# Second-pass attention products in four 32-column tiles, layer-1 sums of 24 batches beside the LSTM, and a reserve of two buffers in a four-layer graph network on one core

## The chip, the core and the metric

The kernel runs on one NeuronCore of a Trainium2 chip. The core has a matrix engine (TensorE, "PE" in the profile, its weight loads apart as "PEld"), VectorE ("DVE"), ScalarE ("ACT"), GpSimd ("POOL"), and a queue of its own for issuing transfers (SyncE, "SP"). [...] The metric is the device time of one launch in microseconds, lower is better. A profile is of one execution; its span is the time from its first to its last instruction.

## The reference

The input is 32 independent graphs ("batches") of 512 nodes with 128 features, each with a symmetric 0/1 adjacency of 512 x 512 that has ones on its diagonal. Four layers follow one another, each as `x = x + layer(relu(layernorm(x)), adj)`:

```
layer 0  q, k, v = relu(h Wq + bq), relu(h Wk + bk), relu(h Wv + bv)
         x += softmax(where(adj, q k^T, -9e15)) v
layer 1  conv   = conv1d(last 128 nodes of h) + bias               # 128 steps of 128 features
         lw     = lstm(conv), 128 steps, run over all 32 batches at once
         A_norm = D^-1/2 (adj + 1) D^-1/2,  D from the row sums of adj + 1
         x += sigmoid((A_norm h) lw)
layer 2  four inner layers on n0 = h:
         n' = tanh([norm_rows(adj)^T (n ws + bs), n wn + bn, norm_cols(adj)^T (n wd + bd)] wu + bu)
layer 3  x += prelu(adj (h W) + bias)
```

The LSTM needs layer 0 of the last 128 nodes of all batches, and everything from layer 1's gate `sigmoid((A_norm h) lw)` on needs the last step of the LSTM. The product `A_norm h` doesn't need it.

## The kernel before, in words

The file holds a general kernel and a fast one (`symmetric`) for symmetric adjacencies; the fast one runs here, and the general one only if a flag at the end says so. What follows is the fast one.

It works in three passes over the 32 batches. **Pass 1** (`pass_1`) does layer 0 for the last 128 nodes of each batch, with the convolution, and stores keys, queries, values and the updated rows in DRAM. **The LSTM** (`lstm`) then runs 128 steps over all batches together; beside it, **pass 2** (`pass_2`) does layer 0 for the other 384 nodes. For the batches in `EARLY` (0 to 19) pass 2 also loads the whole adjacency, squares it on ScalarE (the square of 0/1 entries is the same, and the row sums come with it), and computes layer 1's product `A_norm h` (`sums_of_1`), which it stores in DRAM. **The rest** (`rest`) does, for each batch, the layer-1 gate, layer 2 and layer 3; a batch that isn't early computes its sums of layer 1 there, and an early one loads them into a tile `f_gT3` with the tag "gs". The last four batches (`LATE = 4`) have pass 2 ranked with the rest. Two batches, 26 and 27 (`FIRST`), go first in the rest and keep what pass 2 loaded.

The tiles that the prediction names are: `f_z`, the LSTM's gates before tanh; `f_pq`, `f_s`, `f_e`, `f_po`, pass 2's queries, scores, exponentials and weighted sums; `f_pg`, layer 1's sums (and layer 3's); `f_plw` and `f_pl`, the transposed LSTM output and the product with it (the gate); `f_py`, `f_pa`, layer 2's products, with the node tiles `f_n`; `f_xn`, `f_hT`, a normalized batch and its transposition; `f_dgT` and `f_gT3`, the stored and the loaded sums.

All float32 products of a wide stationary operand use the whole 128 x 128 array. The LSTM's products are different: with 32 batches, h is only 32 columns wide as the stationary operand, so `products` (line 1210) issues four matmuls for one step, each into 32 partitions of the output, that is into a 128 x 32 part of the array ("128*32" in the profile). The sums over the adjacency (`aggregate`, line 1396) run in a reduced float32 format at 512 columns.

The order of the work is not written by hand. Every operation is given to a planner (`Plan`) with an engine, an assumed duration, a rank, and the tiles that it reads and writes; `Plan.run` then places operations one by one where they can start first, with a lower rank first among those that can start at once, and keeps each engine's order as planned. The LSTM's operations have ranks below 1000 and are never to be delayed by others on their engine (`held`). For TensorE the planner adds a pause wherever a tiled and an untiled operation follow each other:

```
SWITCH = (0.2, 0.1)                      # line 536: to untiled, to tiled
s = max(s, free[e] + self.SWITCH[o.tiled])
```

An operation can only be placed when buffers for its new tiles are free (`room`, line 663): for each tag it counts how many the operation needs. "gs" has five buffers, the adjacency "a" two, PSUM ("mm") eight banks. The transfers are issued on SP in the planned order, so a transfer that waits for its buffer holds up those behind it; the copy of the squared adjacency to DRAM is issued on POOL.

Lines that matter: 1292 (`f_pq`), 1301 (`f_s`), 1310 (`f_po`), 1213 (`f_z`), 1349 (squares), 1396 (sums), 1432 (load of `f_gT3`), 775 (`EARLY`).

Of the kernel before, what the change touches and what calls it, by code (L numbers as in the profile page):

```python
# [13 lines left out]
P = 128  # L14
# [478 lines left out]
class Cell:  # L493


    def __init__(self, pool, tag, shape, dtype, name, whole=False, filled=False):
        self.pool, self.tag, self.shape, self.dtype, self.name = pool, tag, shape, dtype, name
        self.whole, self.filled = whole, filled
        self.size = 1
        for n in (shape or ())[1:]:  # L500
            self.size *= n
        self.place = None
        self.marked = True
        self.real = None
        self.left = 0
        self.free_at = 0.0
        self.parts = {}
# [13 lines left out]
class Plan:  # L521
# [74 lines left out]
    def run(self, tc, queues):  # L596
# [66 lines left out]
        def room(o):  # L663

            at = 0.0
            need = {}
            for c in o.cells:
                if c not in seen:
                    if c.tag in self.fifo and self.fifo[c.tag][turn[c.tag] + need.get(c.tag, 0)] is not c:
                        return None  # L670
                    need[c.tag] = need.get(c.tag, 0) + 1
            for t, n in need.items():
                spare = n + (t == self.banks and o.rank >= self.spared and self.left > 0)
                if len(slots[t]) < spare or len(slots[t]) == spare and t in self.kept and by_rank and o.rank > by_rank[-1].rank + 12:
                    return None
                at = max(at, sorted(slots[t])[n - 1])
            return at
# [5 lines left out]
        tiled = False  # L683
# [69 lines left out]
def symmetric(ctx, tc, x, adj, weights, cols, rows, lstm_b, prelu_a, out, fail):  # L753
# [18 lines left out]
    MANY = 512 // (4 * B)  # L772
    LATE = 4
    FIRST = [B - LATE - 2 + k for k in range(2)]
    EARLY = range(20)
    FOLDS = (4, 7, 10, 13)
    MOVED = range(2, B - 2)
    TURN = 32
# [34 lines left out]
    def t_mm(n):  # L813
        return max(0.222, n * 0.001676)
# [449 lines left out]
        return last  # L1264


    def pass_2(b):
        R = 20_000 + b * 10 if b < B - LATE else 30_000 + (b - B + LATE) * 10 + 15
        dkq, dv, dl, dx = kept[b]
# [19 lines left out]
        if whole:  # L1289
            DMA(R, 64, lambda: nc.sync.dma_start(xc.t[:, L, :], dl.t), [dl], [(xc, L)])  # L1290
        pq = bank(f"f_pq_{b}", (P, NR), whole=False)
        PE(R, t_mm(NR), lambda: nc.tensor.matmul(pq.t, w[:, W_Q, :], hT.t, start=True, stop=True), [hT], [pq])
        q = new("xn", (P, NR), f"f_q_{b}")
        plan.op({
            "ACT": (t_act(NR) + 0.09, lambda: nc.scalar.activation(q.t, pq.t, AF.Relu, bias=colb[:, C_Q : C_Q + 1])),
# [2 lines left out]
        es = []  # L1298
        for j in range(NT):
            s = bank(f"f_s_{b}_{j}", (P, NR), whole=False)  # L1300
            PE(R, t_mm(NR), lambda s=s, j=j: nc.tensor.matmul(s.t, keys.t[:, bass.ts(j, P)], q.t, start=True, stop=True),  # L1301
               [keys, q], [s])
            e = new(f"n{j}" if j < 3 else "y", (P, NR), f"f_e_{b}_{j}")
            ACT(R, t_act(NR), lambda s=s, e=e: nc.scalar.activation(e.t, s.t, AF.Exp), [s], [e])  # L1304
            DVE(R, t_dve(NR), lambda e=e, j=j: nc.vector.tensor_mul(e.t, e.t, rows_of(j)), [(mask, j)], [e])
            es.append(e)
        po = bank(f"f_po_{b}", (P, L, P + 1), whole=False)
        for t in range(L):
            for j in range(NT):
                PE(R, t_mm(P), lambda t=t, j=j: nc.tensor.matmul(  # L1310
                    po.t[:, t, :], es[j].t[:, bass.ts(t, P)], v.t[:, j, :], start=(j == 0), stop=(j == NT - 1)),
                    [es[j], v], [po])
        ri = plan.fixed(None)
        sum_ops.append(DVE(R, 0.21, lambda: nc.vector.reciprocal(rinv[:, b, :L], po.t[:, :, P]), [po], [ri]))
        for t in range(L):
# [85 lines left out]
    def rest(b, turn, lw_after):  # L1401
# [27 lines left out]

        if b in EARLY:  # L1430
            gT, first = new("gs", (P, N), f"f_gT3_{b}"), None
            DMA(R, 256, lambda: nc.sync.dma_start(gT.t, kept_sums[b].t), [kept_sums[b]], [gT])
        else:
            gT, first = sums_of_1(R, b, xc, ar, rs)
            diagonal(R, ar, OP.subtract)
# [245 lines left out]
```

## Time and profile before

| | before |
|---|---|
| median of three runs | 1313.07 us (1310.22 to 1316.28) |
| span of the profiled execution | 1311.1 us |
| TensorE busy | 1284.8 us, 98% of the span |
| VectorE, ScalarE, GpSimd busy | 1000.2, 824.9, 388.3 us |
| granted TensorE clock, all stages | 1.00, and 0.97 from 1200 us to the end |
| DMA, mean | 176 GB/s, 230.69 MB |

The profiled execution's own time is its span, 1311.1 us; the median of the runs lies 2.0 us above it. Busy times of TensorE are of modelled ends, so two records that overlap count once, and a busy TensorE isn't one that streams without pause: the distance between the starts of two records says what one really took. One float32 product is two records[...], and one in four tiles is eight; the reduced format takes one.

Pass 1 lies between 0 and 182 us, the LSTM's products between 182 and 502.6 us, and the rest behind that.

### The profile page before, as it was taken

To read this page: it belongs to the slowest core of one execution; us is meant where nothing else is said; L and a number is where in the kernel's file an instruction comes from. 1 tells how busy PE (TensorE), PEld (TensorE's weight loads), DVE (VectorE), ACT (ScalarE), POOL (GpSimd) and SP (SyncE) were. 2 spreads that over 40 slices of the span, in tenths; PEclk is the share of its full clock that TensorE was granted. 3 is DMA by queue.
4 is the path that set the end of the run, shared out by engine and by line. 5 is a ranking of instruction groups with operands and counts; after the bars stand their busy time and mean duration, and the time that the engine had idled before them with its cause. 6 is when DMAs were issued, how large, how long until landed. Compare 5 with 4: busy or idle time off the path is not lost.

```text
span 1311.1 us, 26435 instructions
## 1 busy us (share of the span) xinstructions
PE 1284.8 (98%) x8834; PEld 987.9 (75%) x8834; DVE 1000.2 (76%) x3396; ACT 824.9 (63%) x2084; POOL 388.3 (30%) x729
## 2 busy tenths in 40 slices
PE   9999999999999999999999999999999999999997
PEld 6898876766666667777777777787877877877774
DVE  7998977878788778765588768677777887787754
ACT  5666657777865655675387557575765675675433
POOL 5654433222221123332143224132222332332000
PEclk9999999999999999999999999999999999999999
DMA  8888888887666657885469766866645566673211
GB/s 271 265 273 273 269 275 284 269 277 227 214 214 197 205 160 135 205 213 119 107 151 204 163 153 145 191 146 150 156 122 114 122 137 145 138 169 65 50 31 36
DMA packets 298833, 230.69 MB, mean 176 GB/s; under 512 B 138048, under 2 KB 245824, under 8 KB 298688
## 3 DMA queue, kind: packets, MB, share of 16 engines
q1 hardware_dynamic: 281792, 212.13, 57.6%
q0 software_dynamic: 16896, 16.78, 8.2%
q8 instruction: 72, 1.18, 0.4%
q14 instruction: 73, 0.60, 0.1%
HBM read 135.80 MB, written 61.60 MB: 151 GB/s over the span
## 4 chain that ended last, share of the span: by engine, by line
PE 52%; DVE 2%; ACT 2%; DMA 1%; issue 1%; POOL 1%; SPq 0%; ACTq 0%; DVEq 0%
PE f_pa L1396 16%; PE f_pa L1501 14%; PE f_py L1490 13%; PE f_pg L1396 5%; PE f_p L1542 2%; PE f_pl L1444 2%; DMA f_hT_c<-f_hl_c 1%; ACT f_ar L1349 1%; ACT f_xn_c L1047 0%; DVE f_pa L1497 0%; DVE f_x L1546 0%; ACT f_neg L1545 0%; DVE f_y L1379 0%; DMA f_hT_d<-f_hl_d 0%; POOL f_dinv L1421 0%
## 5 line engine op out<-in xcount | busy, mean ns | idle before, releaser
L1396 PE MATMUL f_pa<-f_ar,f_y 128*128 128x512 f32 x1024 | 292.2, 422 | 0.6 <-ACT f_y L1378 0.6
L1396 PEld LDWEIGHTS f_pa<-f_ar,f_y 128*128 128x128 f32 x1024 | 188.5, 188 | 66.5 <-issue 28.4
L1490 PE MATMUL f_py<-f_wf,f_n 128*128 128x128 f32 x1280 | 173.9, 275 | 0.2 <-ACT f_n L1505 0.2
L1490 PEld LDWEIGHTS f_py<-f_wf,f_n 128*128 128x128 f32 x1280 | 164.0, 192 | 9.4 <-issue 1.9
L1505 ACT ACTIVATE f_n<-f_pa,f_bcol 128x512 f32<-128x512 f32 x128 | 88.1, 690 | 110.3 <-PE f_pa L1501 107.1
L1501 PE MATMUL f_pa<-f_n,f_wf 128*128 128x512 f32 x320 | 152.8, 593 | 1.1 <-DVE f_pa L1497 1.1
L1349 ACT ACTIVATE f_ar<-f_a 128x512 fp32r<-128x512 f32 x208 | 129.3, 624 | 19.1 <-DMA f_a<-in_adj_dram 12.8
L1378 ACT CAST f_y<-f_py 128x512 fp32r<-128x512 f32 x128 | 74.8, 584 | 81.5 <-PE f_py L1490 76.7
L1310 PEld LDWEIGHTS f_po<-f_v,f_e 128*128 128x128 f32 x768 | 100.7, 190 | 23.8 <-issue 11.1
L1497 DVE TENSOR_TENSOR f_pa<-f_pa,f_inv 128x512 f32<-128x512 f32 x128 | 87.4, 693 | 39.4 <-PE f_pa L1396 38.6
L1379 DVE TENSOR_TENSOR f_y<-f_py,f_y 128x512 fp32r<-128x512 f32 x128 | 87.4, 685 | 34.7 <-ACT f_y L1378 34.3
L1310 PE MATMUL f_po<-f_v,f_e 128*128 128x129 f32 x768 | 112.5, 282 | 0.0
L1301 PE MATMUL f_s<-f_q,f_k 128*128 128x384 f32 x256 | 100.1, 501 | 0.0
L1458 POOL DMA_DIRECT2D f_das<-f_ar x32 | 28.8, 899 | 222.4 <-ACT f_ar L1349 125.1
L1501 PEld LDWEIGHTS f_pa<-f_n,f_wf 128*128 128x128 f32 x320 | 56.7, 190 | 44.8 <-issue 36.7
L1213 PE MATMUL f_z<-f_w,f_seq 128*32 128x128 f32 x2040 | 82.3, 278 | 6.2 <-DVE f_seq L1261 4.0
L1463 DVE SCALAR_TENSOR_TENSOR f_junk<-f_a,f_aT 128x1024 bf16<-128x1024 f32 x64 | 78.2, 1221 | 8.4 <-DMA f_aT<-f_das 7.3
L1213 PEld LDWEIGHTS f_z<-f_w,f_seq 128*32 128x32 f32 x2040 | 48.3, 109 | 43.5 <-ACT f_e L1304 8.3
L1396 PE MATMUL f_pg<-f_ar,f_xp_d 128*128 128x512 f32 x256 | 77.4, 426 | 0.3 <-DVE f_xp_d L1387 0.2
L1304 ACT ACTIVATE f_e<-f_s 128x384 f32<-128x384 f32 x128 | 62.0, 488 | 20.4 <-PE f_s L1301 18.7
L1396 PE MATMUL f_pg<-f_ar,f_xp_c 128*128 128x512 f32 x256 | 74.1, 416 | 0.4 <-ACT f_xp_c L1386 0.4
L1490 PE MATMUL f_py<-f_wf,f_T_c 128*128 128x128 f32 x448 | 72.7, 275 | 0.0
(205 smaller groups left out, 2732.5 us busy)
## 6 DMA issues: line engine op xcount, KB each, us to landing
f_a<-in_adj_dram SPq DMA_DIRECT2D x52, 1024.0 KB
f_das<-f_ar POOLq DMA_DIRECT2D x32, 512.0 KB, 5.2
f_dkq<-f_kh SPq DMA_DIRECT2D x32, 448.0 KB
f_dv<-f_v SPq DMA_DIRECT2D x32, 258.0 KB
f_v<-f_dv SPq DMA_DIRECT2D x32, 258.0 KB
f_x<-in_x_dram SPq DMA_DIRECT2D x32, 256.0 KB
f_al<-in_adj_dram SPq DMA_DIRECT2D x32, 256.0 KB
f_k<-f_dkq SPq DMA_DIRECT2D x32, 256.0 KB
```

Of the source, the lines that this page charges most:

```text
L1213: nc.tensor.matmul(z.t[part, k, :, :], h, w[:, m : m + 4, part], start=False, stop=True, skip_group_check=True)
L1301: PE(R, t_mm(NR), lambda s=s, j=j: nc.tensor.matmul(s.t, keys.t[:, bass.ts(j, P)], q.t, start=True, stop=True), [keys, q], [s])
L1310: PE(R, t_mm(P), lambda t=t, j=j: nc.tensor.matmul(po.t[:, t, :], es[j].t[:, bass.ts(t, P)], v.t[:, j, :], start=(j == 0), stop=(j == NT - ...
L1349: ACT(rank, 0.62, lambda t=t: nc.scalar.activation(ar.t[:, t, :], a.t[:, t, :], AF.Square, accum_out=deg.t[:, t : t + 1]), [a], [(ar, t), ...
L1378: ACT(rank, t_act(N), lambda: nc.scalar.copy(parts.t[:, :, 0, :], src.t), [src], [(parts, 0)])
L1379: DVE(rank, t_dve(N), lambda: nc.vector.tensor_sub(parts.t[:, :, 1, :], src.t, f32(parts.t[:, :, 0, :])), [src, (parts, 0)], [(parts, 1)])
L1396: nc.tensor.matmul(pg.t, parts.t[:, j, k, :], ar.t[:, j, :], start=(k == 0 and j == 0), stop=(k == 1 and j == NT - 1))
L1463: nc.vector.scalar_tensor_tensor(junk, flat(a.t[:, 2 * k : 2 * k + 2, :]), 1.0, flat(aT.t[:, 2 * k : 2 * k + 2, :]), OP.mult, OP.not_equal ...
L1490: nc.tensor.matmul(py.t[:, j, :], nodes[n].t[:, bass.ts(j, P)], wf[:, W_F[i] + c, 0, :], start=False, stop=(c == nch - 1), skip_group_chec ...
L1497: before = DVE(R, t_dve(N), lambda pa=pa: nc.vector.tensor_mul(pa.t, pa.t, inv_row.t), [inv_row], [pa])
L1501: nc.tensor.matmul(pa.t, wf[:, W_F[i] + c, 1, :], nodes[n].t, start=False, stop=(c == nch - 1), skip_group_check=True)
L1505: ACT(R, 0.57, lambda pa=pa, n=n, i=i: nc.scalar.activation(n.t, pa.t, AF.Tanh, bias=bcol[:, i : i + 1]), [pa], [n])
```

## The change

Three edits. The float32 products of pass 2 (`f_pq`, `f_s`, `f_po`) are each issued as four matmuls of 32 stationary columns into four groups of 32 partitions, and are marked as tiled for the planner. `EARLY` goes from 20 to 24 batches, so batches 20 to 23 load the whole adjacency in pass 2, square it, and compute and store their sums of layer 1 there; in the rest they load them. A cell gets a number `ahead`, which `room` adds to the count of free buffers that it asks for: the loads of `f_gT3` now start only when three "gs" buffers are free, and leave two.

```diff
@@ class Cell
         self.place = None
+        self.ahead = 0
@@ Plan.run, room
             need = {}
+            ahead = 0
             for c in o.cells:
                 if c not in seen:
+                    ahead = max(ahead, c.ahead)
...
-                spare = n + (t == self.banks and o.rank >= self.spared and self.left > 0)
+                spare = n + ahead + (t == self.banks and o.rank >= self.spared and self.left > 0)
@@ symmetric
-    EARLY = range(20)
+    EARLY = range(24)
...
+    def quarters(product):
+        for k in range(P // TURN):
+            product(slice(k * TURN, (k + 1) * TURN))
@@ pass_2
-        PE(R, t_mm(NR), lambda: nc.tensor.matmul(pq.t, w[:, W_Q, :], hT.t, start=True, stop=True), [hT], [pq])
+        PE(R, t_mm(NR), lambda: quarters(lambda p: nc.tensor.matmul(pq.t[p], w[:, W_Q, p], hT.t, start=True, stop=True)), [hT], [pq], tiled=True)
...
-            PE(R, t_mm(NR), lambda s=s, j=j: nc.tensor.matmul(s.t, keys.t[:, bass.ts(j, P)], q.t, start=True, stop=True),
-               [keys, q], [s])
+            PE(R, t_mm(NR), lambda s=s, j=j: quarters(lambda p: nc.tensor.matmul(
+                s.t[p], keys.t[:, j * P + p.start : j * P + p.stop], q.t, start=True, stop=True)), [keys, q], [s], tiled=True)
...
-                PE(R, t_mm(P), lambda t=t, j=j: nc.tensor.matmul(
-                    po.t[:, t, :], es[j].t[:, bass.ts(t, P)], v.t[:, j, :], start=(j == 0), stop=(j == NT - 1)),
-                    [es[j], v], [po])
+                PE(R, t_mm(P), lambda t=t, j=j: quarters(lambda p: nc.tensor.matmul(
+                    po.t[p, t, :], es[j].t[:, t * P + p.start : t * P + p.stop], v.t[:, j, :], start=(j == 0), stop=(j == NT - 1))),
+                    [es[j], v], [po], tiled=True)
@@ rest
             gT, first = new("gs", (P, N), f"f_gT3_{b}"), None
+            gT.ahead = 2
```

The planner's assumed durations of the products stay as they were; what it sees of the tiles is that the pause between an LSTM step and a product of pass 2 falls away, and its order on every engine changes with that.

## The prediction

> **What bounds the kernel now.** I read the page first: TensorE is busy nearly all the time, and the chain that ended last is mostly TensorE.
>
> ```profile
> span 1311.1 us, 26435 instructions
> ...
> PE 1284.8 (98%) x8834; PEld 987.9 (75%) x8834; DVE 1000.2 (76%) x3396; ACT 824.9 (63%) x2084; POOL 388.3 (30%) x729
> ...
> PE 52%; DVE 2%; ACT 2%; DMA 1%; issue 1%; POOL 1%; SPq 0%; ACTq 0%; DVEq 0%
> ```
>
> Matmul ends are modelled, so I take TensorE's cost from the distance between starts instead, stage by stage. The table of stretches, cut where the LSTM's products begin and end, has the columns stretch, length, then busy time and count of PE, PEld, DVE, ACT, POOL, then clock, DMA share, GB/s:
>
> ```profile
> 0.00:182.00 182.00, 176.45 (x1288) 150.91 (x1288) 156.69 (x690) 113.67 (x228) 94.22 (x248) 1.00 0.86 272
> 182.00:502.60 320.60, 314.29 (x3253) 218.91 (x3253) 256.79 (x1174) 222.78 (x776) 78.88 (x151) 1.00 0.71 224
> 502.60:1311.10 808.50, 794.02 (x4294) 618.09 (x4294) 586.70 (x1535) 488.48 (x1080) 215.16 (x331) 1.00 0.60 135
> ```
>
> The change works in the middle stage, 128 LSTM steps with the second pass between them. The timeline of TensorE there (start, length, line, tile, records; a float32 product is two records, four tiles make eight):
>
> ```profile
> 220.17 0.64 PE L1213 MATMUL f_z<-f_w,f_seq 128*32 128x128 f32 x16
> 220.75 2.05 PE L1310 MATMUL f_po<-f_v,f_e 128*128 128x129 f32 x16
> 222.73 0.64 PE L1213 MATMUL f_z<-f_w,f_seq 128*32 128x128 f32 x16
> ...
> 230.17 0.64 PE L1213 MATMUL f_z<-f_w,f_seq 128*32 128x128 f32 x16
> ...
> 304.53 1.38 PE L1310 MATMUL f_po<-f_v,f_e 128*128 128x129 f32 x10
> 305.75 0.49 PE L1003 MATMUL f_bT<-f_ident,f_rowb 128*128 128x128 f32 x3
> ...
> 499.45 0.42 PE L1213 MATMUL f_z<-f_w,f_seq 128*32 128x128 f32 x8
> 499.81 0.49 PE L1310 MATMUL f_po<-f_v,f_e 128*128 128x129 f32 x2
> 500.14 2.10 PE L1301 MATMUL f_s<-f_q,f_k 128*128 128x384 f32 x6
> 502.17 0.43 PE L1213 MATMUL f_z<-f_w,f_seq 128*32 128x128 f32 x8
> ```
>
> Eight f_z records last 499.81 - 499.45 = 0.36 us to the next start, sixteen 220.75 - 220.17 = 0.58. So a tiled product streams in 0.22, and 0.14 is fixed per visit. Ten f_po records take 1.22, two take 0.33: 0.111 a record, 0.222 a product, and 0.11 once behind f_z. Sixteen f_po that end at f_z take 1.98: 16 x 0.111 + 0.11 + 0.09. One visit of the LSTM to TensorE thus costs 0.14 + 0.11 + 0.09 = 0.34 beyond streaming; from the same starts unrounded, 0.33. f_s: (2.03 - 0.09) / 6 = 0.323 a record, 0.646 a product. The waits of the weight loads in this stage show part of it as idle time of 0.2 us behind nearly every step:
>
> ```profile
> PEld f_po L1310 <- issue: 10.1, 51, 0.2
> PEld f_pg L1396 <- issue: 5.2, 26, 0.2
> PEld f_s L1301 <- issue: 4.6, 22, 0.3
> ```
>
> [...] here four f_z tiles stream 16 records in 0.44, the rate of a wide f_po[...], though for 128 columns only. [...] f_po's 0.111 a record with a 0.190 load each says that they overlap here.
>
> **The check of the sum.** From the order of instructions I added, step by step, what stands on TensorE between two LSTM steps: 0.222 a product of f_po, 0.646 of f_s and f_pq, 0.22 of f_z, 0.231 for each 512-wide f_pg (16 f_pa of that shape take 3.68 in the chain), 0.33 a visit. Before, all 127 intervals hold one visit: 269.0 of products + 127 x 0.33 = 310.9 us. Measured, first to last f_z: 502.17 - 182.09 = 320.1. Most single steps agree to 0.05 (220.17 to 222.73 is 2.56; the sum is 2.56). The rest is a floor: where the sum is less than about 2.2, the step waits for its own chain of tanh and cell, and the short steps last 2.14 to 2.4. With a floor of 2.25 the sum is 313.6, and 6.5 are left: 1.5 in the first step, the others where ACT or DVE was held by something else. Behind the LSTM TensorE waits for almost nothing: the seven largest waits of that stage sum to 4.6. So the kernel is TensorE's work, and a change is worth what it takes from it.
>
> **The change, part by part.**
>
> Tiles. Each of 32 f_pq, 128 f_s and 384 f_po becomes four products of 32 columns. Streaming: no change at 0.646 and 0.222, as f_z shows for four tiles; the work concerned is 160 x 0.646 + 384 x 0.222 = 188.6 us, on which an unknown percentage falls. I take zero; from f_z, -2% to +2%; the rival below prices more. Visits: in the order after, 81 of 126 intervals between LSTM steps hold no change of mode and 45 hold one (f_pg and the folds are still wide). With 6.3 us more products within the stage (351 f_po and 124 f_s done by its end, against 348 and 119), it is 275.3 + 45 x 0.33 = 290.2. But now 35 steps have less than 2.2 on TensorE and 50 lie between 2.2 and 2.4, so the floor counts: with 2.25 it is 300.1, and with the same 6.5 on top 306.6. Change: -13.5.
>
> Ahead of the LSTM: 2.0 us fewer products, but eight visits to tiled second-pass products (8 x 0.33 = 2.6): +0.5. Behind it: 4.6 fewer products, two more visits: -3.9.
>
> 24 early batches. The order shows 168 f_pg products before the last LSTM step in both, and 344 after: the sums of batches 21 to 23 slip behind the LSTM, so TensorE gains nothing here. Added for batches 20 to 23: sixteen squares on ACT (0.62 + 0.19 each, 13 us, in a stage where ACT is busy 223 of 321), 4 x 0.68 of diagonals moved earlier on DVE, powers on POOL (79 of 321). On SP's queue: 256 KB more adjacency, 64 KB of x, 256 KB of sums stored and later 256 KB loaded, each; 2.3 MB in a stage with a DMA share of 0.71. All hidden by TensorE's products; in a stage of 306 I estimate DVE at 87% and ACT at 79%, which is why I keep the 6.5 of disturbances rather than shrink them. Uncovered, the squares alone would be 13 us; f_e's exponentials queue behind them on ACT, and f_po behind f_e.
>
> Loaded sums. A load of f_gT3 now needs three free "gs" buffers. What is late next is f_plw, first of its batch on TensorE. In the order after, the steady loads stand 37.7 us of TensorE work ahead of f_plw; so this costs nothing, unless a landing takes six times the 3 to 6 us that the transposing transfers f_hT_c take in the chain.
>
> The hand-over. Right behind the last step the order after puts five sums (9.2 us), and batch 26 then has only 6.2 us of products between its gates f_pl and its first f_py, against 11.7 before, where the real distance was 12.5 (507.6 to 520.1). Its shortest chain, from row durations (four tanh, update, statistics, power, normalization, transposition, eviction), is about 8. So 2 to 6 us idle; in its first layers nothing stands between f_py, sums and the next layer, another 4 or so (one wait each of about 1.0, 1.1, 0.8, 1.2). That is 7 to 8 against 3.2 measured before in three waits (0.5, 1.6, 1.1): +4, from 0 to +7.
>
> Sum: -13.5 + 0.5 - 3.9 + 4 = -13 us. Against the profiled execution's own span, 1298; the median of the three runs lies 2.0 above that span, so 1300.
>
> **The rivals.** (a) The LSTM chain binds more than I think: a floor of 2.4 (DVE and ACT fuller) gives 307.9 + 6.5 = 314.4, a gain of 5 in all, 1308. For it: some short steps do last 2.3 to 2.46. [...] (b) [...] 290 + 7, and no idle hand-over: -27, 1286. (c) Slower: long tiled streams lose rate. [...] It decides from 13 / 188.6 = 7% on. Against: f_z's four tiles; for: no run here shows 384 columns in tiles. (d) Slower through instruction supply: if the queue of 72 packets (1.18 MB) is TensorE's, a packet holds 17668 / 72 = 245 records; 6500 more records are 27 more packets, and the LSTM stage would take one every 6 us instead of 12. A wait of 0.25 us on each of some 50 would cancel the gain; 1 us would give 1350. [...]
>
> **How the numbers follow.** My forecast has 0.63 (own range 1292 to 1307), (a) 0.14, (b) 0.10, (c) 0.07, (d) 0.06. A measurement of this kernel tells about 0.5% (6.6 us) from no change: faster is below 1306.5. The forecast, (b) and a third of (a) are faster, 0.78; the rest of (a) and the mild forms of (c) and (d), 0.12; 0.10 slower. The range reaches from (b), 1286, to the top of (a) and the mild forms of (c) and (d), 1314.
>
> **What would show it.** Right: f_po at 0.22 a product of eight records, f_s at 0.65; the 0.2 us "issue" waits fall from some 100 to some 45; first to last f_z 300 to 312 us; idle TensorE of 5 to 9 us in the 45 us behind the LSTM. Wrong: f_s over 0.69 in tiles, gaps that recur every 245 records, steps that wait on DVE or ACT at 2.4 throughout.

## The result, and the profile after

The changed kernel takes 1324.03 us (median of seven runs, 1319.14 to 1327.30), the kernel before 1315.38 on the same chips (1310.22 to 1316.83): a ratio of 1.0068, with a 95% interval of 1.0050 to 1.0087. It is slower by 0.7%, where 1300 was forecast; the time lies 10 us above the range. The profiled execution's span is 1322.7 us.

The page of the changed kernel, with the busy times, the queue of instructions (packets, MB, share of 16 DMA engines) and the shares of the chain that ended last:

```profile
span 1322.7 us, 32990 instructions
...
PE 1274.2 (96%) x12098; PEld 977.1 (74%) x12099; DVE 990.9 (75%) x3392; ACT 847.3 (64%) x2116; POOL 392.8 (30%) x737
...
q8 instruction: 98, 1.61, 0.5%
...
PE 84%; DMA 5%; DVE 5%; ACT 2%; issue 2%; POOL 1%; SPq 1%; ACTq 0%; POOLq 0%; DVEq 0%
```

TensorE is busy for 10.6 us less than before, and yet the kernel is longer. The queue that was there with 72 packets has 98. The stretches, cut as for the kernel before where the LSTM's products begin and end (same columns):

```profile
0.00:182.00 182.00, 177.63 (x1404) 147.98 (x1404) 153.79 (x684) 114.13 (x228) 92.94 (x245) 1.00 0.85 272
182.00:513.20 331.20, 305.26 (x6205) 212.12 (x6198) 265.61 (x1203) 237.62 (x830) 89.10 (x167) 0.99 0.68 214
513.20:1322.70 809.50, 791.30 (x4501) 617.01 (x4498) 571.50 (x1506) 495.50 (x1059) 210.74 (x325) 0.99 0.62 141
```

The first stretch is as before, the last 1.0 us longer. The loss is in the middle one: 331.2 us against 320.6, of which TensorE is idle for 26 where it was idle for 6. From first to last `f_z` it is 182.16 to 512.83, 330.7 us, and the prediction said 306.6.

The tiles themselves cost what was forecast. The timeline of TensorE in this stage:

```profile
347.51 2.15 PE L1308 MATMUL f_s<-f_q,f_k 128*32 128x384 f32 x24
349.45 0.65 PE L1216 MATMUL f_z<-f_w,f_seq 128*32 128x128 f32 x16
349.89 0.85 PE L1308 MATMUL f_s<-f_q,f_k 128*32 128x384 f32 x8
350.54 0.42 PE L1317 MATMUL f_po<-f_v,f_e 128*32 128x129 f32 x8
350.76 0.85 PE L1308 MATMUL f_s<-f_q,f_k 128*32 128x384 f32 x8
```

Three products of `f_s` take 349.45 - 347.51 = 1.94, 0.647 each; one of `f_po` takes 350.76 - 350.54 = 0.22; and the two products of `f_z` between take 349.89 - 349.45 = 0.44, 0.22 each, with none of the 0.33 of a change of mode. What takes the time is seen elsewhere in the same view. The bracket at a line's end is the idle time before it and what ended it:

```profile
304.84 0.62 PE L1216 MATMUL f_z<-f_w,f_seq 128*32 128x128 f32 x16
305.27 1.95 PE L1317 MATMUL f_po<-f_v,f_e 128*32 128x129 f32 x63
309.24 0.27 PE L1317 MATMUL f_po<-f_v,f_e 128*32 128x129 f32 x1 [2.01 <-issue]
```

In the middle of a run of 64 `f_po` records, operands there, nothing to wait for, TensorE stands still: the 63rd record starts at 306.95, the 64th at 309.24. A packet of the instruction queue starts at 306.68. Two more such pauses, of 2.28 us at 422.7 and 2.57 at 435.8, end 2.4 us after the start of an instruction packet, and two shorter ones (0.79 and 0.93 us) end 2.5 and 2.4 after one. The stage's four other pauses of 1.8 us and more are of another kind: their next instruction waits for ACT or DVE. Around the one that ends at 294.31, `f_z` waits for the LSTM's output on DVE, this for a tanh on ACT, and the tanh stood there behind a square that waited for the adjacency (who waited, for what: total, times, longest):

```profile
DVE f_h L1263 <- ACT f_tcn L1259: 3.0, 2, 2.3
ACT f_ar L1356 <- DMA f_a<-in_adj_dram: 2.5, 1, 2.5
...
PE f_z L1216 <- DVE f_seq L1264: 2.0, 1, 2.0
```

The waits of the whole stage, of after and below of before:

```profile
PEld f_z L1216 <- issue: 13.8, 24, 2.6
ACT f_ar L1356 <- DMA f_a<-in_adj_dram: 11.0, 7, 3.3
PEld f_po L1317 <- issue: 10.4, 35, 2.3
...
PE f_po L1317 <- issue: 6.1, 7, 2.0
DVE f_x L1047 <- DMA f_dx<-f_x: 5.6, 6, 2.1
ACT f_x L1050 <- DMA f_dx<-f_x: 4.5, 3, 2.7
```

```profile
DVE f_x L1044 <- DMA f_dx<-f_x: 4.5, 5, 1.2
ACT f_ar L1349 <- DMA f_a<-in_adj_dram: 4.3, 4, 2.4
ACT f_x L1047 <- DMA f_dx<-f_x: 3.0, 2, 1.6
```

The many short "issue" waits became fewer, but some of 2 us came, and the three groups in which ACT and DVE wait for transfers sum to 21.1 us instead of 11.8. A tanh or a cell of the LSTM that stands behind such a wait on its engine is late with it, as the tanh was around 294.31, where `f_h` waited up to 2.3 us for it.

A third loss shows in the same timeline. For 3.4 us from 324.4 on, and again from 396.1 on, the granted clock of TensorE was 0.5; before had none of this in the stage. In the first, three products of `f_po` took 326.30 - 324.79 = 1.51, or 0.50 each in place of 0.22:

```profile
324.79 1.58 PE L1317 MATMUL f_po<-f_v,f_e 128*32 128x129 f32 x24
326.30 1.89 PE L1403 MATMUL f_pg<-f_ar,f_xp_c 128*128 128x512 f32 x4
```

At this rate the 6.8 us cost some 3.4, an estimate. The two stretches begin 0.2 and 1.2 us after pauses of 2.68 and 2.52 us had ended (from one start of a matmul to the next), but four other pauses of over 2 us (2.25, 2.28, 2.28 and 2.57) weren't followed by one.

Two causes, then, offer themselves. **S, supply**: a tiled product is eight records with their weight loads in the time of two, and TensorE's instructions come as packets over a DMA queue (q8, 98 packets where before has 72). **D, data**: transfers that arrive late for ACT and DVE. And a third, **O**: the order that the planner makes for tiled products is worse in itself.

### The profile page after: what moved, and what is told of

The parts are those of the page before. It is cut to its first block, busy times and chain, and to the rows that moved or that the text cites. A ratio compares the mean times of both kernels' runs of the same rounds, so it can differ in the third digit from the quotient of the medians.

```text
span 1322.7 us, 32990 instructions
## 1 busy us (share of the span) xinstructions
PE 1274.2 (96%) x12098; PEld 977.1 (74%) x12099; DVE 990.9 (75%) x3392; ACT 847.3 (64%) x2116; POOL 392.8 (30%) x737
## 3 DMA queue, kind: packets, MB, share of 16 engines
q8 instruction: 98, 1.61, 0.5%
## 4 chain that ended last, share of the span: by engine, by line
PE 84%; DMA 5%; DVE 5%; ACT 2%; issue 2%; POOL 1%; SPq 1%; ACTq 0%; POOLq 0%; DVEq 0%
PE f_pa L1403 18%; PE f_py L1498 15%; PE f_pa L1509 15%; PE f_pg L1403 8%; PE f_s L1308 5%; PE f_po L1317 4%; PE f_z L1216 3%; DMA f_a<-in_adj_dram 3%; PE f_p L1550 2%; PE f_pl L1452 2%; PE f_pk L1123 2%; PE f_pv L1139 2%; PE f_sl L1156 2%; PE f_pol L1166 2%; PE f_pq L1299 1%
## 5 line engine op out<-in xcount | busy, mean ns | idle before, releaser
L1403 PE MATMUL f_pa<-f_ar,f_y 128*128 128x512 f32 x1024 | 300.5, 430 | 5.3 <-DVE f_y L1386 4.5
L1498 PEld LDWEIGHTS f_py<-f_wf,f_n 128*128 128x128 f32 x1280 | 165.5, 192 | 11.2 <-ACT f_n L1513 1.9
L1356 ACT ACTIVATE f_ar<-f_a 128x512 fp32r<-128x512 f32 x224 | 138.6, 621 | 19.5 <-DMA f_a<-in_adj_dram 18.3
L1317 PE MATMUL f_po<-f_v,f_e 128*32 128x129 f32 x3072 | 108.5, 277 | 8.3 <-issue 6.1
L1317 PEld LDWEIGHTS f_po<-f_v,f_e 128*32 128x32 f32 x3072 | 91.0, 111 | 20.8 <-issue 10.4
L1308 PE MATMUL f_s<-f_q,f_k 128*32 128x384 f32 x1024 | 99.8, 488 | 0.1
L1216 PEld LDWEIGHTS f_z<-f_w,f_seq 128*32 128x32 f32 x2040 | 54.9, 109 | 56.0 <-issue 13.8
L1403 PE MATMUL f_pg<-f_ar,f_xp_d 128*128 128x512 f32 x256 | 74.4, 413 | 0.3 <-DVE f_xp_d L1394 0.2
L1078 DVE COPY f_hl_d<-f_n 128x1024 uint16<-128x1024 uint16 x28 | 19.4, 693 | 71.2 <-ACT f_n L1513 71.2
```

The lines of the kernel that those rows point to most:

```text
L1216: nc.tensor.matmul(z.t[part, k, :, :], h, w[:, m : m + 4, part], start=False, stop=True, skip_group_check=True)
L1308: PE(R, t_mm(NR), lambda s=s, j=j: quarters(lambda p: nc.tensor.matmul(s.t[p], keys.t[:, j * P + p.start : j * P + p.stop], q.t, start=Tru ...
L1317: PE(R, t_mm(P), lambda t=t, j=j: quarters(lambda p: nc.tensor.matmul(po.t[p, t, :], es[j].t[:, t * P + p.start : t * P + p.stop], v.t[:, ...
L1356: ACT(rank, 0.62, lambda t=t: nc.scalar.activation(ar.t[:, t, :], a.t[:, t, :], AF.Square, accum_out=deg.t[:, t : t + 1]), [a], [(ar, t), ...
L1403: nc.tensor.matmul(pg.t, parts.t[:, j, k, :], ar.t[:, j, :], start=(k == 0 and j == 0), stop=(k == 1 and j == NT - 1))
L1498: nc.tensor.matmul(py.t[:, j, :], nodes[n].t[:, bass.ts(j, P)], wf[:, W_F[i] + c, 0, :], start=False, stop=(c == nch - 1), skip_group_chec ...
```

## The experiments

All stages below are measured from first to last `f_z`. The sum is that of the prediction (products, 0.33 a change of mode, a floor of 2.25 a step). The excess is the stage less its sum. In the prediction, and in the expectations of same_order_wide, tiles_ahead20 and scores_tiled, two LSTM steps with nothing between them were counted as one, 1.8 us too little; in several later expectations a step that other products split was counted twice. The table has each of the 127 intervals once, and its sums differ from the expectations' by up to 1.8 us.

"At edges" needs a word. The packets of the instruction queue hold 16 KB each (1.61 MB in 98), and behind the LSTM there is one for every 254 to 256 of TensorE's instructions (see "How late the packets are" below). If TensorE really runs out of them, its pauses must stand at every 256th instruction and nowhere else. They do: with TensorE's instructions counted in the traces (matmuls, weight loads and the waits of its queue), the pauses at 306.95, 422.7 and 435.8 stand exactly behind instruction 449 + 256 n. In the changed kernel's stage 22 distances between successive instructions exceed 0.6 us; six stand at these edges, and these six are the only ones whose next instruction waits for no semaphore. In the stages of the other kernels, too, every distance over 0.65 us without such a wait stands at one of these edges. The column sums the distances over 0.15 us at edges, where the next instruction starts under 3.1 us after the start of the next packet. "Data waits" are the waits of ACT and DVE for transfers, all groups. "Half clock" is time at a granted clock of 0.5. All are of the LSTM stage, in us. They overlap, and not every us of a wait reaches TensorE, so they needn't add up to the excess. Each ratio is to the kernel before in the same series (medians 1312.68 to 1315.38).

| run | changes of mode | sum | stage | excess | at edges | data waits | half clock | median us | ratio to before (95%) |
|---|---|---|---|---|---|---|---|---|---|
| before | 127 | 313.6 | 320.1 | 6.5 | 0 | 12.2 | 0 | 1315.38 |  |
| after | 45 | 301.9 | 330.7 | 28.8 | 10.6 | 21.7 | 6.8 | 1324.03 | 1.0068 (1.0050 to 1.0087) |
| same_order_wide | 126 | 324.8 | 332.6 | 7.8 | 0 | 15.3 | 0 | 1327.33 | 1.0119 (1.0084 to 1.0154) |
| before_order_tiled | 58 | 300.0 | 324.5 | 24.5 | 9.9 | 16.4 | 3.4 | 1329.14 | 1.0128 (1.0091 to 1.0165) |
| tiles_ahead20 | 41 | 302.1 | 329.1 | 27.0 | 13.3 | 15.8 | 6.8 | 1330.77 | 1.0143 (1.0114 to 1.0171) |
| sums24_ahead_only | 127 | 313.5 | 323.3 | 9.8 | 0 | 12.6 | 0 | 1315.89 | 1.0024 (1.0008 to 1.0040) |
| before_light_adj | 127 | 313.6 | 321.5 | 7.9 | 0 | 4.3 | 0 | 1316.73 | one run |
| before_light_tiled | 58 | 300.0 | 315.1 | 15.1 | 3.1 | 0.7 | 0 | 1310.47 | one run |
| scores_tiled | 92 | 311.6 | 336.8 | 25.2 | 0 | 18.9 | 13.7 | 1334.84 | 1.0149 (1.0118 to 1.0181) |
| po_tiled | 101 | 305.2 | 318.8 | 13.6 | 0.8 | 18.5 | 0 | 1334.00 | 1.0154 (1.0126 to 1.0182) |
| after_dma260 | 46 | 304.5 | 316.9 | 12.4 | 8.9 | 1.1 | 1.5 | 1326.14 | 1.0089 (1.0063 to 1.0116) |
| tiles20_dma260 | 42 | 302.3 | 316.2 | 13.9 | 8.8 | 1.6 | 1.9 | 1320.16 | 1.0053 (1.0039 to 1.0068) |
| after_split_adj | 43 | 303.5 | 320.9 | 17.4 | 11.2 | 3.4 | 0 | 1308.42 | 0.9963 (0.9946 to 0.9980) |
| before_order_mid_tiled | 70 | 302.4 | 329.1 | 26.7 | 3.5 | 23.8 | 6.8 | 1324.03 | 1.0065 (1.0040 to 1.0091) |
| before_split_adj | 127 | 310.4 | 318.2 | 7.8 | 0 | 7.3 | 0 | 1327.48 | 1.0114 (1.0094 to 1.0134) |
| split_wide_same_order | 128 | 328.6 | 329.7 | 1.1 | 0 | 0.8 | 0 | 1316.58 | 1.0033 (1.0021 to 1.0044) |
| after_p2dma260 | 48 | 304.2 | 318.2 | 14.0 | 12.0 | 3.3 | 0 | 1313.58 | 1.0002 (0.9988 to 1.0017) |
| after_split_p2dma260 | 50 | 302.3 | 316.1 | 13.8 | 7.9 | 0 | 0 | 1304.12 | 0.9929 (0.9909 to 0.9948) |

**Order and tiles taken apart.** The first run keeps the changed kernel's order on every engine and issues wide products; the second keeps the order of before and issues tiles. Their edits, the first against the changed kernel, the second against the one before:

```diff
-                PE(R, t_mm(P), lambda t=t, j=j: quarters(lambda p: nc.tensor.matmul(
-                    po.t[p, t, :], es[j].t[:, t * P + p.start : t * P + p.stop], v.t[:, j, :], start=(j == 0), stop=(j == NT - 1))),
+                PE(R, t_mm(P), lambda t=t, j=j: nc.tensor.matmul(
+                    po.t[:, t, :], es[j].t[:, bass.ts(t, P)], v.t[:, j, :], start=(j == 0), stop=(j == NT - 1)),
                     [es[j], v], [po], tiled=True)
```

```diff
-                PE(R, t_mm(P), lambda t=t, j=j: nc.tensor.matmul(
-                    po.t[:, t, :], es[j].t[:, bass.ts(t, P)], v.t[:, j, :], start=(j == 0), stop=(j == NT - 1)),
+                PE(R, t_mm(P), lambda t=t, j=j: quarters(lambda p: nc.tensor.matmul(
+                    po.t[p, t, :], es[j].t[:, t * P + p.start : t * P + p.stop], v.t[:, j, :], start=(j == 0), stop=(j == NT - 1))),
                     [es[j], v], [po])
```

`f_pq` and `f_s` are treated likewise in both. The mark for the planner stays as it was in each, and with it the plan.

> The changed kernel with its order of work and its transfers kept (each engine's instructions stand in the same order), but every product of f_pq, f_s and f_po issued as one wide product again: 13,096 matmul instructions in place of 14,728, and a real change of mode at 126 of 126 steps. By the same sum as in the prediction the LSTM stage is 275.7 + 126 x 0.33 = 317.3, 323.0 with the floor of 2.25. Theory S (supply of TensorE's instructions is what the tiles starve): the pauses of 2.2 us that wait for nothing vanish, the disturbances are back near 6.5, stage 328 to 333, whole kernel about 1322 to 1326, no slower than the changed kernel [...]. Theory D (the 24 batches' transfers and squares hold the steps, whatever TensorE's instructions are): the 30 us of disturbances stay, stage about 350, whole kernel about 1343.

> The kernel before with its order of work, its 20 batches and its transfers kept, but the products of f_pq, f_s and f_po issued as four tiles. 58 changes of mode are left in the LSTM stage; the sum is 268.6 + 58 x 0.33 = 287.7, 300.0 with the floor. Theory S: pauses of about 2.2 us without a releaser appear here too, with nothing else changed; disturbances of 20 to 30 in place of 6.5, stage 320 to 330, whole kernel 1315 to 1325. Theory D: disturbances stay at 6.5, stage 306, whole kernel about 1301. Theory O (the order that the planner makes of tiled products is what is bad): also 1301.

The stages came out as S has them, 332.6 and 324.5 us; the medians lie 1.3 and 4.1 us above its ranges, in the second because tiles stand among wide products ahead of the LSTM and behind it (a later run takes this up). With wide products in the changed order the excess is 7.8; with tiles in the old order, with the old transfers, it is 24.5. D would have kept some 30 in the first, D and O 6.5 in the second. The timeline of the second shows the pause where the changed kernel's order has no part in it (an instruction packet starts at 374.89):

```profile
374.48 0.65 PE L1315 MATMUL f_po<-f_v,f_e 128*32 128x129 f32 x14
377.18 0.30 PE L1315 MATMUL f_po<-f_v,f_e 128*32 128x129 f32 x1 [2.06 <-issue]
```

and the wait of the first for its `f_po` loads is the old short one only:

```profile
PEld f_po L1317 <- issue: 8.3, 42, 0.2
```

So the tiles bring the excess, with the same order and the same transfers. Not all of it is supply: of the changed kernel's 28.8 us, 10.6 stand at edges, where all the kernels with wide products have none, and the data waits grew from 15.3 to 21.7. The changed order has a price too: issued wide it sums to 324.8 for 275.7 of products, the old one to 313.6 for 269.0, 4.5 more beyond the products; it is only worth having if the tiles pay. In this order they pay 332.6 - 330.7 = 1.9 us of 22.9.

**The parts of the change.** `EARLY = range(20)` with tiles and the two free buffers; and 24 batches with the two free buffers and without tiles. (The free buffers were not tried alone.)

> The change with the layer 1 sums of 20 batches instead of 24: tiles and the two free buffers stay. The sum for the LSTM stage is 277.9 + 41 x 0.33 = 291.4, 300.3 with the floor. Theory S: about the changed kernel, stage 325 to 331, whole 1318 to 1325. Theory D: disturbances near 6.5 again, stage 307, whole 1301 to 1304.

> The change without the tiles: sums of 24 batches and two free buffers, products wide and planned as wide. The sum for the LSTM stage is 268.6 + 127 x 0.33 = 310.6, 313.5 with the floor. Theory S: disturbances 6.5 to 10, stage 320 to 324, whole kernel 1314 to 1319. Theory D: disturbances of 25 to 30, stage about 340, whole about 1335.

Again S: without the four batches the tiles lose as much (excess 27.0), and the batches without tiles cost 0.24%, 3 us, all of it in the stage (9.8 of excess). The median of the first, 1330.77, lies 5.8 above what was expected at most, though its stage lies within it; its profiled span is 1323.6.

**Less data.** If it is the data that makes packets late, they must come sooner with less of it. Most of the second pass's adjacency is left out in a pair with the order of before: the data queue moves 45.9 MB in the stage in place of 70.9 (the expectations have 22 MB less; it is 25), and its share falls from 70.1% to 46.2% and, in tiles, 47.7%.

```diff
-            DMA(R, 1024, lambda: nc.sync.dma_start(a.t, adj[b].rearrange("(t p) j -> p t j", p=P)), [], [a])
+            if b < 4:
+                DMA(R, 1024, lambda: nc.sync.dma_start(a.t, adj[b].rearrange("(t p) j -> p t j", p=P)), [], [a])
+            else:
+                POOL(R, 0.1, lambda: nc.gpsimd.memset(flat(a.t)[:, P:], 1.0), [], [(a, "ones")])
+                DMA(R, 1024, lambda: nc.sync.dma_start(a.t[:, 0, :P], adj[b, :P, :P]), [], [(a, "loaded")])
```

The 768 KB load of the batches that aren't whole is cut likewise; before_light_tiled issues tiles besides.

> The kernel before in its own order, with most of the second pass's adjacency left out: from the fifth early batch on, and for the batches that load 768 KB, only 128 rows by 128 columns (64 KB) are loaded and the rest of the tile is set to 1 by GpSimd, 22 of the 71 MB that the LSTM stage moves. The values are not those of the reference. The sum for the LSTM stage is unchanged, 313.6 with the floor; it is the measure for the next run. All theories: stage 316 to 320, whole kernel 1306 to 1312.

> The same with the products of f_pq, f_s and f_po issued as four tiles, the order still that of before; the same adjacency is left out. The sum for the LSTM stage is 300.0 with the floor. Theory S-late (the instruction packets arrive late because they stand behind data on the DMA engines): with 22 MB less the pauses of 2.2 us go or become few, stage 304 to 310, whole kernel 1293 to 1303, against 324.5 and 1325 for the tiles with full adjacency. Theory S-rate (TensorE can't be fed at this rate of records whatever the data): the pauses stay, stage 318 to 325, whole 1310 to 1320.

Wide, the data made no difference (321.5 against 320.1). In tiles the stage falls from 324.5 to 315.1, and the long pauses are gone. The waits of before_light_tiled for TensorE's own issue (before_order_tiled has 2.3, 1.6 and 1.4 as the longest):

```profile
PEld f_po L1320 <- issue: 13.3, 55, 0.9
PEld f_s L1310 <- issue: 12.8, 57, 1.1
PEld f_z L1213 <- issue: 10.8, 32, 1.0
```

The time at edges falls from 9.9 to 3.1 us, so most of it goes with the data. Neither expectation held in full: S-rate's pauses went, but S-late's 304 to 310 was not reached. An excess of 15.1 stays where the wide twin has 7.9; the 3.1 at edges are part of this difference of 7.2, and what the other 4 are isn't shown. Each of the two ran once, and their values are not the reference's; the comparison is of their stages.

**How late the packets are.** Behind the LSTM the packets come, on average, every 254 to 256 of TensorE's instructions, in all these kernels. The earliest packets of the LSTM stage start at instruction 175 + 256 n before, and three instructions ahead of that after. Measured from 175 + 256 n, the packets of the LSTM stage start 2.6 us late on average before and 2.9 after, 5.4 and 6.8 at worst. That is much the same in time; but before it is 127 instructions at worst, and in the changed kernel 274, which is 449 - 175, the place where its pauses stand. At the edges the next instruction never started less than 2.18 us after its packet did, in any kernel; in those with wide products throughout it was 5.8 us or more, and their time at edges is 0. With less data the tiled twin's median delay falls from 3.9 to 1.9 us. The counts of packets in the stage, of after and of before (q1 is the data):

```profile
q1 hardware_dynamic: 51093, 69.78, 67.1%
q8 instruction: 49, 0.80, 1.0%
```

```profile
q1 hardware_dynamic: 52673, 70.88, 70.1%
q8 instruction: 26, 0.43, 0.5%
```

So packets are late beside data and less late with less of it (3.9 and 1.9 us); on which DMA engine, and behind what, no view shows.

**Fewer tiles.** `f_pq` and `f_s` alone tiled and planned so, and `f_po` alone, both with 20 batches and without free buffers.

> Tiles for f_pq and f_s alone (planned and issued so), f_po wide, sums of 20 batches, no free buffers asked for. A tiled f_s takes 16 records with its loads in 0.65 us, so 256 records last 10 us; f_po in tiles took 16 in 0.22, 256 in 3.6 us. 92 changes of mode in the LSTM stage; sum 309.9 with the floor for 275.1 of products, against 313.6 for 269.0 before, so 6 us of products come out of the time behind the LSTM. Theory S-late: no pauses of 2 us, disturbances 6.5 to 10, stage 316 to 320, whole kernel 1300 to 1307, which would beat both kernels. If any tile brings the pauses: 1312 to 1320.

> Tiles for f_po alone (planned and issued so), f_pq and f_s wide, sums of 20 batches, no free buffers asked for. 101 changes of mode; sum 305.2 with the floor for 265.1 of products (3.9 us of products less than before move behind the LSTM). Theory S-late: the dense runs of f_po records bring the pauses back, disturbances 12 to 22, stage 317 to 327, whole kernel 1312 to 1322. If the number of added records over the whole stage were all that counts, disturbances of about 16. If tiles are harmless: stage 312, whole 1307.

Both missed, and each for a reason of its own. Scores in tiles have 34 packets and no pause at an edge, as expected, but an excess of 25.2: in this order single steps of 4.5 to 7.2 us wait for transfers, and 13.7 us of the stage ran at half clock. The waits of DVE and ACT in its LSTM stage:

```profile
DVE f_x L1047 <- DMA f_dx<-f_x: 9.4, 5, 2.8
ACT f_x L1050 <- DMA f_dx<-f_x: 7.4, 3, 2.8
```

So D is real as well, and here it came with a new order. `f_po` in tiles had 0.8 us at an edge, far less than S had for its dense records; its stage (318.8) is near the lower end, but behind the LSTM it takes 831.1 us where 813 were due: its six largest waits there, all for ACT and DVE, sum to 15.1 us, where before the seven largest sum to 4.6. A new plan can lose 15 us anywhere.

**Time for the transfers.** If D holds the other half, transfers planned further ahead, or let go in smaller pieces, should remove it. The planner's price of a transfer, and the early batches' load:

```diff
-        return 0.1 + kb / 315.0
+        return 0.1 + kb / 260.0
```

```diff
-            DMA(R, 1024, lambda: nc.sync.dma_start(a.t, adj[b].rearrange("(t p) j -> p t j", p=P)), [], [a])
+            for t in range(NT):
+                DMA(R, 256, lambda t=t: nc.sync.dma_start(a.t[:, t, :], adj[b, t * P : (t + 1) * P, :]), [], [(a, t)])
...
-                                                             accum_out=deg.t[:, t : t + 1]), [a], [(ar, t), (deg, t)])
+                                                             accum_out=deg.t[:, t : t + 1]), [(a, t)], [(ar, t), (deg, t)])
```

The first edit is that of after_dma260 and, with `EARLY = range(20)`, of tiles20_dma260; the second that of after_split_adj. before_order_mid_tiled is before_order_tiled with tiles for batches 3 to 26 alone.

> The changed kernel with one constant of its planner changed: a transfer is planned at 260 KB per us in place of 315, so the planner sets transfers further ahead of the work that reads them. Tiles, 24 batches and two free buffers stay; 46 changes of mode, sum 295.4, 306.2 with the floor for 280.3 of products (floor less products 25.9, against 24.8 in the changed kernel and 44.6 before). Theory L (about half of the 24 us lost is instruction packets late, the other half steps held by ACT or DVE that wait for data transfers): the second half shrinks, excess over the sum 15 to 22 in place of 30.6; stage 321 to 328 with 5 us more products in it, whole kernel 1309 to 1316. If the loss is all instruction packets: excess about 30, whole kernel 1324.

> The same planning price of 260 KB per us with tiles, two free buffers and the sums of 20 batches. 42 changes of mode, 304.1 with the floor for 277.9 of products. Theory L: as the run beside it with 3 us less, stage 318 to 325, whole 1307 to 1314. If all is instruction packets: stage 332, whole 1325.

> The changed kernel with the early batches' adjacency loaded in four transfers of 256 KB, each released to its own square, in place of one of 1 MB. 43 changes of mode, 304.9 with the floor for 280.0 of products. If the square's wait for the whole megabyte is what holds ACT (11.0 us of waits in the changed kernel): those waits fall below 4, excess over the sum 20 to 24, whole kernel 1314 to 1318. [...]

> The kernel before in its own order with the products of f_pq, f_s and f_po of batches 3 to 26 alone issued in tiles, those that run mostly inside the LSTM stage; 70 changes of mode, 302.4 with the floor. The run with all batches in tiles lost 3 us ahead of the LSTM and 7 behind it. If those came from tiles that stand among wide products there: the LSTM starts at 182 to 183 again and what is behind it takes 809 to 811; stage 322 to 327, whole kernel 1313 to 1319.

The price does in the stage what L said, and more: the excess is 12.4 and 13.9, of which 8.9 and 8.8 stand at edges, and the data waits of ACT and DVE fall from 21.7 us to 1.1 and 1.6. The whole kernel didn't gain: the LSTM starts at 194.1 and 194.4 in place of 182.2. The first pass is planned with the same price, and a later run takes this up. The quarters take the waits of the three groups from 21.1 to 3.4 us (0.9 for the square), more than I expected, and give the first kernel that is faster than before: 1308.42. The pauses at edges stay, 11.2 us, up to 2.8 each. In before_order_mid_tiled the 3 and 7 us outside the stage came back (it starts at 183.4, and 809.7 us follow), but the stage is worse, 329.1, with 23.6 us of such data waits: same order, same transfers, 19 packets more than before, but only 3.5 us at edges. In three pairs with full data and whole loads (before and before_order_tiled, 12.2 to 16.4; before and this run; same_order_wide and the changed kernel) the data waits grew as tiles were put into a fixed order, by a chain that I did not follow.

**Whose gain it is.** The last four runs: the quarters in the kernel before; the 1308 us kernel with wide products in its own order; the price for ranks from 20,000 on alone; and both remedies.

```diff
-        return plan.op({"SP": (max(0.45, t_dma(kb)), fn)}, rank, r, w, gap=k.pop("gap", 2.0), **k)
+        return plan.op({"SP": (max(0.45, 0.1 + kb / (260.0 if rank >= 20_000 else 315.0)), fn)}, rank, r, w, gap=k.pop("gap", 2.0), **k)
```

> The kernel before, without any part of the change, with the early batches' adjacency loaded in four transfers of 256 KB. 127 changes of mode, 310.4 with the floor for 262.4 of products (floor less products 48.0, before 44.6). If the quarters alone made the 1308 us, this run is near 1306 too. If the tiles made it, once the data waits were out of their way: the kernel before had only 6.5 us of disturbances to lose; stage 314 to 317, behind it 813 to 818, whole kernel 1310 to 1317.

> The 1308 us kernel (change and quarters) with its order of work and transfers on every engine kept, products of f_pq, f_s and f_po issued wide: 128 changes of mode in place of 43, 329.6 with the floor in place of 304.9. Measured with tiles: excess 18.3, 11 of it after instruction packets. Expected wide: no such pauses, excess 4 to 8, stage 334 to 338, whole kernel 1319 to 1324: the tiles would then be worth 11 to 16 us in this order, against 3 in the changed kernel's. If the pauses don't come from the tiles' records: excess 15 to 18, whole 1331.

> The changed kernel with transfers planned at 260 KB per us in the second pass and behind it alone; the first pass is planned as before. 48 changes of mode, 304.2 with the floor for 280.8 of products. Expected: the LSTM starts at 182 to 183 again; waits of ACT and DVE for data in the LSTM stage below 5 us in all; excess 10 to 16; stage 314 to 320, behind it 802 to 812, whole kernel 1299 to 1313. If excess is over 20 the price does not do it and the earlier run was luck.

> Quarters and the planning price of the second pass together. 50 changes of mode, 303.7 with the floor for 276.0 of products. The two remedies act on the same waits, so they don't add: excess 10 to 16, nearly all of it after instruction packets, stage 314 to 320, behind it 805 to 812, whole kernel 1302 to 1313.

The quarters alone make the kernel before slower (its new plan loses behind the LSTM, 824.2 us). Against its wide twin the 1308 us kernel's tiles are worth 329.7 - 320.9 = 8.8 us of stage, and 8.2 between medians of two series: the changes of mode saved are worth 25.1, the excess gives 16.3 back, 11.2 of it at edges, and the wide twin has none there. I had expected 11 to 16. The price for the second pass alone left the median where the kernel before has it (1.0002), with an excess as expected but the LSTM starting at 186.4, so the price in the first pass was 8 of the 12 us there. That run's 14.0 of excess are 12.0 at edges and 2.0 others. Both together give the best kernel, 1304.12 us, 0.9929 of before with an interval of 0.9909 to 0.9948, and faster than both kernels of this document. Its stretches:

```profile
0.00:179.70 179.70, 175.02 (x1388) 147.68 (x1388) 152.76 (x676) 112.86 (x226) 94.45 (x245) 1.00 0.84 267
179.70:496.40 316.70, 305.46 (x6204) 208.14 (x6204) 268.53 (x1220) 235.74 (x822) 89.04 (x167) 1.00 0.72 229
496.40:1303.50 807.10, 791.84 (x4517) 616.94 (x4506) 573.11 (x1507) 492.53 (x1059) 210.65 (x325) 0.99 0.62 141
```

TensorE's busy time in the stage is that of the changed kernel, to 0.2 us; the stage is 14.5 us shorter. In the five kernels with tiles and data waits under 3.5 us, apart from the pair with little data, what is left of the excess beyond the edges is 2.0 to 6.2 us, where the kernel before has 6.5.

## Why the prediction was wrong

- **The cost of the tiles: right.** 0.647 for `f_s` and 0.22 for `f_po`, against 0.646 and 0.222 wide: no loss of rate in tiles of 384 columns; rival (c), a loss that no run had shown, is out.
- **The changes of mode: right.** Between the LSTM's products and tiled ones the timeline has none of the 0.33 us, and the sum of the wide twin of the 1308 us kernel, with 128 changes at that price, misses its stage by 1.1 us only. The 0.33 is a measured time; what TensorE does in it no view shows.
- **The sum for the stage, 300.1, is nearly right; the term on top of it failed.** The sum took 126 intervals for 127: between 267.87 and 270.08 two LSTM steps follow each other with nothing between them, and with a floor for this one it is 301.9. "With the same 6.5 on top 306.6" took the disturbances of another order and another rate of instructions as a constant. They measured 28.8: 10.6 at the edges of packets, some 3.4 at half clock (an estimate), and most of the rest behind late data, to judge by the fall to 12.4 once the transfers had time. The step behind it, "all hidden by TensorE's products", is the one that failed for the data: ACT waited 11.0 us for the adjacency, and the LSTM's tanh behind it. No view of the kernel before could show what a new plan's transfers do; its own 11.8 us of such waits were in the waits, and I left them unread because the products covered most of them.
- **Rival (d) named another part, and was under-rated.** Its count was right (26 packets more; one per 6.7 us in the stage), its form nearly: not every packet waits, but the 10.6 us at edges are 0.22 on each of 49 packets, next to the 0.25 that it gave as enough to cancel the gain. The sign that the text named, gaps that recur every 245 records, was the right one to look for, with 256 instructions in its place. What the text missed is how to price it from the profile before: there a packet is already up to 127 instructions late, and with twice the instructions in the same time this comes to some 254, an estimate, next to the 274 at which TensorE stood still in the changed kernel.
- **Ahead of the LSTM and behind it: right.** +0.1 us at the start of the LSTM for +0.5; +0.9 behind it for +0.1 (-3.9 and +4). TensorE is idle for 7.3 us in the 45 us behind the LSTM (busy 37.7), for the 7 to 8 forecast; some luck is in it, since 4.5 of that are one wait (`f_pa` for `f_y` on DVE) and not the several short ones that were added up.
- **24 batches and the free buffers at nothing: nearly.** Without tiles they cost 3 us (0.24%, from 0.08 to 0.40%).
- **The floor, rivals (a) and (b): (b) didn't happen.** Its 290 + 7, a stage without the floor, was my estimate, and no trace had shown a reason for it. (a)'s floor of 2.4 would add 7.8 us to the changed kernel's sum. The 2.0 to 6.2 us that other kernels with tiles have left leave little room for it, but no run sets the floor apart.

Left open: some 4 us of the excess that tiles keep with little data, why data waits grow when tiles alone are put into a fixed order, and why the granted clock fell to 0.5 where it did.

## What to carry to other kernels

Count the instructions a stage issues per microsecond, as well as their time: the edit here, which splits each product in four, left the cost of `f_s` and `f_po` unchanged (0.647 us against 0.646, 0.22 against 0.222) and still brought 10.6 us of pauses at packet edges, in a stage with a DMA share of 0.68. The count of instructions per packet (256 here), with how late packets start before (up to 127 instructions), could have warned of it. Whether a pause is one of supply can be told by counting: in these traces such pauses (six of 0.67 to 2.57 us in the changed kernel) stood 256 instructions apart, or a multiple of it, with no semaphore behind them. The disturbances left over after a sum belong to the order and the transfers of that kernel; they don't carry over to a new plan, so read the waits for data in it as the first term at risk. If a plan is made from prices, give the transfers room first, and judge a TensorE edit then.

## What the runs showed of the hardware

- In the LSTM stage a TensorE instruction packet of 16 KB took 1.09 us on average in the changed kernel, 1.04 in the kernel before. Where TensorE stood at the edge of one, it went on 2.2 to 3.1 us after the next one's start (in the changed kernel 2.3 to 2.6). The pauses stand 274 instructions behind the point at which the earliest packets start, to within three instructions. Before, with packets late by 127 instructions at most, the time at edges is 0.
- In the changed kernel's LSTM stage the granted clock was 0.5 for 3.4 us in two places, 0.2 and 1.2 us behind pauses of 2.68 and 2.52 us; a product of `f_po` then took 0.50 us in place of 0.22. That the pauses caused it isn't shown.
- Four column tiles of 32 stream 384 columns at the wide rate: 0.647 us a float32 product (changed kernel) against 0.646 (before).
